# The tail of a graph network kernel: float16 halves, turns by products, 12 open output sums, tables added by DMA

## The chip, the cores and the metric

One NeuronCore of a Trainium2 chip runs the whole program as one launch. Its engines run beside each other and wait for each other through semaphores: TensorE (PE; its weight loads are listed as PEld), VectorE (DVE), ScalarE (ACT), GpSimd (POOL) and SyncE (SP, which here only issues transfers). TensorE writes to PSUM, a memory of 8 banks; the other data lie in SBUF, and large tables in DRAM. The metric is device time in microseconds (us). The time before is 2712.86 us, the median of three runs (2703.21 to 2717.07).

## The reference

A graph has N = 3125 nodes with 96 features and E = 100000 edges, sorted by destination. Four layers each add to x what they compute from h = relu(layernorm(x)): ten propagation hops (layer 0), a softmax-weighted neighbour sum and a product with W (layer 1), a message network with batch norms over the edges and a sum by destination (layer 2), and two graph convolutions (layer 3). The end of layer 2 and layer 3 are, in short:

```python
message = relu(concat(x[row], x[col], edge_feat) @ W_msg + b_msg)
mu = mean(message, 0); var = mean((message - mu)**2, 0)       # over the edges
message = g_msg * (message - mu) * rsqrt(var + 1e-5) + beta_msg
x = x + segment_sum(message, col) + node_feat

h = relu(layernorm(x))
dinv = rsqrt(deg)                     # in-degree plus the self loop
conv(h, W, b) = segment_sum((h @ W)[src] * dinv[src] * dinv[dst], dst) + b
t = conv(h, W1, b1); t = where(t > 0, t, a1 * t)
x = x + conv(t, W2, b2)
```

## The kernel before

**Tiles and tables.** The 3125 nodes are 25 blocks of 128 rows (`NB` = 25, `P` = 128), 3200 with padding. The counts of edges between all pairs of nodes are built once, as an 8-bit table in SBUF (`C8`, read as float8 `B8`, and its transpose `A8` for layer 0). A propagation or neighbour sum is then a matrix product: for each output block, 25 products of a 128x128 piece of the table with 192 columns of features. The 192 columns are a float16 number and a float16 remainder (`split`: the high half by ACT, the low half by DVE), which together stand for one float32 feature. The table is scaled, which the constant `FINE` = 512 undoes.

**Layers 0 to 2.** Layer 0 runs ten such products (`gather`, L400 on; its matmul is L409). At its end the pool "late" opens (from about L700): SP issues the weights of layers 1 and 2 one after the other, DVE fills a row of ones in `hTs` (L747), POOL writes an index pattern `li` (L761). Layer 1 (loop over the 25 blocks) runs two sums per block (L816), divides them, turns and multiplies by W1, and prepares the node tables `Pt` and `Qt` in DRAM; beside it the edge records are turned into fields (`in_fields`). Layer 2 then runs over units of four times 128 edges: edge features into the buffers `eh` and `el` (L1062 to L1065), messages (L1082), sums by destination (L1111, L1132), which go to one of two tables in DRAM, `Sd[0]` and `Sd[1]`, and a 97x194 product sum `gram` (L1100), from which come the mean and the mean square of the messages. That loop's order is written out by hand (`manual_schedule`). Everywhere else a planner orders the instructions of each engine: it takes the source's order as priority, has its own costs, and lets ready work go ahead of work that waits. It also keeps engines apart by whole PSUM banks: a write to a bank waits for earlier reads of that bank by other engines, whatever columns they touch.

**The tail, before.** After the loop `gram` is copied to `gs` (L1176). The pool "l3" takes SBUF that the message stage used, so its first tiles wait for that stage's last transfers. Then:

- the degree factor `dv` = rsqrt(degree + 1) for all nodes (L1185), by a bit trick and three Newton steps (`rsqrt`, L128 to L133);
- `sd` and `sd2`, the two tables, loaded by SP in five pieces of five blocks each (L1193) and added by POOL (L1194);
- the batch norm's mean and variance by four float32 products with ones (L1206, L1208), some ten DVE operations, a root, the factor `gr` and the shift `sh`;
- for five blocks at a time: the tables times `gr`, the shift times the degree, both added to x, and a layer norm (`norm`, L383 to L389), then per block `normed` (L394) and `weigh`: turn by a float32 transpose (L1227), copy (L1229), product with the float32 weight (L1231), scaled copy to `us` (L1232), and split into `u` (L398, L399);
- `gather` with `conv1` on each pair of output blocks: three DVE operations join the halves, the node's own feature (`us`) and the bias (L1238 to L1241), two make the leaky relu, then `weigh` with the second weight, and x gets the second bias (L1252);
- `gather` with `conv2`, which adds x and sends the block out (L1259).

Each PSUM tile "hop" is one bank and takes two output blocks, which are read after both have been summed. The pool of "hop" has three banks, "zp" and "op" two each.

## Time and profile before

| | |
|---|---|
| profiled execution, its own time | 2710.35 us |
| its span, first to last instruction | 2708.0 us |
| mean granted TensorE clock | 0.857 of full speed |
| busy share of the span | PE 68%, PEld 55%, DVE 55%, ACT 34%, POOL 32% |
| layer 1, about | 1575 to 1745 us |
| layer 2's edge loop, about | 1750 to 2532 us |
| set-up of layer 3 | 2532 to 2558 us |
| features of the 25 blocks | 2558 to 2586 us |
| first gather with conv1 | 2586 to 2651 us |
| second gather with conv2 | 2651 to 2702 us, last output landed by 2708 |

A row of a timeline gives the start, the duration, the engine, the line and operation, the tile written and the tile read, and in brackets how long the engine stood idle before it and what released it. A row of groups gives the busy time and the mean duration in ns, and behind the second bar the idle time of that engine ahead of those instructions. A duration includes a latency that the next independent instruction does not wait for, so starts are closer together than durations are long. A granted clock below 1 slows TensorE's products in proportion.

### The profile page before, as it was taken

The page shows a single profiled execution, that of the slowest core. Times are in us where ns is not written, and L with a number is a line of the kernel's source. Part 1 is how long each engine was busy: PE and PEld are TensorE (multiplying, and loading weights), DVE is VectorE, ACT ScalarE, POOL GpSimd, SP SyncE. Part 2 cuts the span into 40 slices and gives each one's busy share as a digit, 9 for nine tenths or more (in the row PEclk, how much of TensorE's full clock was granted, in tenths as well). Part 3 has the DMA queues.
Part 4 walks back from the last instruction along what each step waited for, and adds up shares of the span by engine and source line. Part 5 has one row for each costly group of instructions (what it writes and reads, how often), then busy time and mean ns, then how long its engine had stood idle before and what let it go on. Part 6 is the DMA issues. An engine that isn't in the chain of part 4 may idle for free. (4 is left out here: it accounts for less than half of the span.)

```text
span 2708.0 us, 51385 instructions
## 1 busy us (share of the span) xinstructions
PE 1844.3 (68%) x19447; PEld 1485.3 (55%) x19447; DVE 1480.2 (55%) x4400; ACT 919.6 (34%) x2334; POOL 870.8 (32%) x928
## 2 busy tenths in 40 slices
PE   0477777871375119314999989768777778788698
PEld 0223335760164008103999978656666666677588
DVE  3778999870045007101664677645655555556853
ACT  0488847370065003001331254223333323223340
POOL 4100000027723770774000000165555555545000
PEclk9889999985588559656999999878999989889799
DMA  4100000000000000000010021134344444334200
GB/s 119 56 9 1 1 1 3 8 10 4 4 9 9 4 4 10 5 4 5 11 26 2 2 51 34 34 95 103 93 106 103 104 101 102 92 95 96 60 1 20
DMA packets 133737, 108.21 MB, mean 40 GB/s; under 512 B 93607, under 2 KB 103341, under 8 KB 133479
## 3 DMA queue, kind: packets, MB, share of 16 engines
q1 hardware_dynamic: 106117, 79.60, 11.2%
q0 software_dynamic: 25952, 22.03, 4.4%
q8 instruction: 154, 2.52, 0.4%
q10 hardware_dynamic: 1410, 3.20, 0.4%
q14 instruction: 104, 0.85, 0.1%
HBM read 86.43 MB, written 18.29 MB: 39 GB/s over the span
## 5 line engine op out<-in xcount | busy, mean ns | idle before, releaser
L409 PE MATMUL hop<-u,A 128*128 128x192 f16 (+1 forms) x6250 | 618.1, 253 | 403.1 <-issue 398.5
L409 PEld LDWEIGHTS <-A 128*128 128x128 fp8e4 x6250 | 542.7, 99 | 492.2 <-issue 470.3
L1024 POOL DMA_INDIRECT h<-Pt,srow x408 | 418.0, 1024 | 505.2 <-PE pre L1082 226.5
L635 DVE SCALAR_TENSOR_TENSOR wt<-hop,sc,h 128x96 f32<-128x96 f32 x225 | 69.7, 310 | 575.6 <-remote 472.5
L555 POOL DMA_INDIRECT recs<-rec,x x250 | 245.6, 982 | 265.1 <-DVE wt L637 182.9
L668 ACT ACTIVATE eps<-eps 96x512 f32<-96x512 f32 x196 | 107.0, 570 | 586.8 <-remote 410.1
L1085 DVE SCALAR_TENSOR_TENSOR u<-pre,u 128x384 f16<-128x384 f32 x216 | 119.5, 553 | 327.6 <-ACT u L1084 267.0
L1084 ACT ACTIVATE u<-pre 128x384 f16<-128x384 f32 x216 | 105.9, 490 | 511.9 <-remote 204.7
L286 PE MATMUL cps<-hk,hl 128*128 128x500 f16 x784 | 231.3, 417 | 61.5 <-DVE hl L244 39.9
L1082 PE MATMUL pre<-W3h,eh 96*128 96x96 f16 x1728 | 230.5, 215 | 17.4 <-issue 17.3
L244 DVE TENSOR_TENSOR hk<-ki,keyT 128x4000 f16<-128x4000 f16 x98 | 219.7, 2242 | 35.7 <-PE cps L286 30.5
L1100 PE MATMUL gram<-u 128*97 128x194 f16 x864 | 200.4, 261 | 26.3 <-issue 25.8
L290 ACT ACTIVATE C<-cps 128x500 f32 x269 | 162.8, 605 | 99.5 <-PE cps L289 67.2
L1082 PE MATMUL pre<-W3h,el 96*128 96x96 f16 x864 | 184.6, 214 | 9.4 <-issue 9.0
L286 PEld LDWEIGHTS <-hl 128*128 128x128 f16 x784 | 73.7, 119 | 169.1 <-DVE hl L244 79.6
L555 POOL DMA_INDIRECT recs<-rec,addr x126 | 123.5, 981 | 106.9 <-DVE x L685 65.5
L1082 PEld LDWEIGHTS <-eh 96*128 96x128 f16 x1728 | 140.2, 103 | 22.2 <-issue 21.8
L1100 PEld LDWEIGHTS <-u 128*97 128x97 f16 x864 | 116.5, 135 | 64.8 <-issue 52.9
L1065 DVE SCALAR_TENSOR_TENSOR el<-ef,eh 96x512 f16<-96x512 f32 x216 | 147.5, 683 | 7.4 <-ACT eh L1064 5.9
L669 DVE BATCH_NORM_STATS2 x<-eps 96x6 f32<-96x512 f32 x196 | 134.5, 687 | 19.3 <-ACT eps L668 10.7
L1064 ACT ACTIVATE eh<-ef 96x512 f16<-96x512 f32 x216 | 126.7, 587 | 23.1 <-DMA spread<-fields 9.8
L1082 PE MATMUL pre<-qa,ohS 128*128 128x96 f16 x912 | 121.2, 210 | 14.5 <-issue 14.1
(427 smaller groups left out, 3738.4 us busy)
## 6 DMA issues: line engine op xcount, KB each, us to landing
spread<-fields SPq DMA_DIRECT2D x114, 256.0 KB
spread<-rl_d SPq DMA_DIRECT2D x51, 256.0 KB
h<-Pt,srow POOLq DMA_INDIRECT x408
recs<-rec,x POOLq DMA_INDIRECT x250
et<-fields SPq DMA_DIRECT2D x228, 9.0 KB
x<-ea_d SPq DMA_DIRECT2D x195, 18.0 KB
qg<-Qt SPq DMA_DIRECT2D x204, 12.0 KB
Sd<-zero SPq DMA_DIRECT2D x2, 1296.0 KB
```

The source lines that it names most:

```text
L244: V.tensor_tensor(t, pat[:, None, :, :].to_broadcast([P, s, n, c]), val[:, q, :].rearrange("p (s c) -> p s c", s=s)[:, :, None, :].to_broa ...
L286: T.matmul(ps, hl[:, j // 4, :, j % 4], hk[:, j // 2, :, j % 2], start=j == js[0], stop=n == 0 and j == js[-1])
L290: S.activation(C8[:, :, bass.ds(column_of(g), WIN)], ps, AF.Copy)
L409: T.matmul(ps[:, i, :], table[:, k, c0 + (b0 + i) * P:c0 + (b0 + i + 1) * P], u[:, k, :], start=k == 0, stop=k == NB - 1)
L555: ins = G.indirect_dma_start(out=recs[g], out_offset=bass.IndirectOffsetOnAxis(ap=addr[:, c0 + c:c0 + c + 1], axis=0), in_=r[:, c, :], in_ ...
L669: V.bn_stats(stats[:, i % 49, :], ps)
L1024: G.indirect_dma_start(out=pgs[i % len(pgs)][:, c, :], out_offset=None, in_=Pt, in_offset=bass.IndirectOffsetOnAxis(ap=srow[:, k:k + 1], a ...
L1064: S.activation(eh, ps[:D, :], AF.Relu)
L1065: V.scalar_tensor_tensor(el, ps[:D, :], 0.0, eh, ALU.max, ALU.subtract)
L1082: T.matmul(ps[:, c, :], t, w, start=j == 0, stop=j == len(by) - 1)
L1085: V.scalar_tensor_tensor(mm[:, :, D + 2:], ps, 0.0, mm[:, :, :D], ALU.max, ALU.subtract)
L1100: T.matmul(gram, mm[:, c, :D + 1], mm[:, c, :], start=n == 0 and c == 0, stop=n == L - 1 and c == HC - 1)
```

## The change

It concerns layer 3 and what leads to it.

- The weights, biases and slope of layer 3 are loaded at the start of layer 1, and the two weights are split into float16 halves there, in a pool that closes at the end of layer 1. The degree factor, its multiples (`dvF` = 512 dv, `dv2` = dv squared), two batch-norm constants (`cc`) and a scaled identity (`own`) are computed in layer 1, too. The memset of `hTs` goes from DVE to POOL.
- `eh` and `el` have two buffers instead of three; `gs` uses one of them.
- Mean and mean square come from one product of 192 columns; the three DVE operations ahead of it stand right behind the copy of `gram`.
- SP loads only `Sd[0]`; a transfer issued by POOL, which adds to what is there, brings `Sd[1]`. POOL's additions and `sd2` are gone.
- `weigh` splits the block before the turn: high half by ACT or DVE in turn, low half by DVE, two float16 products with an identity, one copy of 256 columns, three float16 products (high by high, high by low, low by high), then the high half of `u` by ACT and the low half by DVE, straight from PSUM. There is no `us` any more. Turn and result share one bank, of which there are two.
- The node's own feature: in the first convolution by one more product per output block with the scaled identity (`own`), 26 instead of 25; in the second one DVE operation in `weigh` adds it to x.
- `conv` is one ACT and one DVE operation, `conv1` adds the bias on DVE, `conv2` adds x on DVE; the second bias is added to x in `conv2`.
- The pool of "hop" has six banks. The first 12 output blocks have all their sums open at once (two per bank, started by a product with zeros), and each takes the products of feature block k right after that block's features are queued, one block late. After the last feature block come `conv1` of those 12, then the other 13 blocks, and the second gather, block by block: `done` is called after each block, not after each pair.
- The first group of blocks is of one block, the next of four, the rest of five.

```diff
-    V.memset(hTs[D:, :], 1.0)
+    G.memset(hTs[D:, :], 1.0)
+    soon = ExitStack()
+    where.append(soon.enter_context(tc.tile_pool(name="l1e", bufs=1)))
+    Wg = [load("W_g1", [D, D], a["L3_gnn_W1"]), load("W_g2", [D, D], a["L3_gnn_W2"])]
+    where.pop()
+    bg = [spread("L3_gnn_b1"), spread("L3_gnn_b2")]
+    a1 = spread("L3_gnn_a1", 1)
+    Wgh = [[where[-1].tile([D, D], F16, name=f"W_g{k}{i}") for k in "hl"] for i in range(2)]
+    for (hi, lo_), w in zip(Wgh, Wg):
+        split(hi, lo_, w)
...
+    V.tensor_scalar(own, ident16, 1.0 / FINE, None, ALU.mult)
...
+        V.tensor_scalar(dv, cnt_dst, 1.0, None, ALU.add)
+        V.tensor_copy(dv, rsqrt(dv, "rs_dv"))
+        V.tensor_scalar(dvF, dv, FINE, None, ALU.mult)
+        V.tensor_mul(dv2, dv, dv)
...
-            eh, el = (wp.tile([D, HC * P], F16, name=name) for name in ("eh", "el"))
+            eh, el = (wp.tile([D, HC * P], F16, name=name, bufs=2) for name in ("eh", "el"))
...
         V.tensor_copy(gs, gram)
+        V.scalar_tensor_tensor(mvar[:D, :], gs[:D, D + 2:], 2.0, gs[:D, :D], ALU.mult, ALU.add)
+        V.tensor_mul(sq[:D, D:], mvar[:D, :], ident[:D, :D])
+        V.tensor_add(sq[D:, :D], gs[D:, :D], gs[D:, D + 2:])
...
         for b in range(0, NB, 5):
-            for t, d in ((sd, Sd[0]), (sd2, Sd[1])):
-                nc.sync.dma_start(t[:, b:b + 5, :], d[b * P:(b + 5) * P].rearrange("(b p) d -> p b d", p=P))
-            G.tensor_tensor(sd[:, b:b + 5, :], sd[:, b:b + 5, :], sd2[:, b:b + 5, :], ALU.add)
+            t, d0, d1 = sd[:, b:b + 5, :], *(d[b * P:(b + 5) * P].rearrange("(b p) d -> p b d", p=P) for d in Sd)
+            nc.sync.dma_start(t, d0)
+            nc.gpsimd.dma_start(out=t, in_=d1, accum_op=ALU.add)
...
+        T.matmul(ps, ones[:D + 1, :], sq, start=True, stop=True)
...
         def weigh(i, b, t):
-            zp = qp.tile([P, P], F32, name="zp")[:D, :]
-            T.transpose(zp, t, ident)
-            zT = wp.tile([D, P], F32, name="zT")
-            S.activation(zT, zp, AF.Copy)
-            op = qp.tile([P, D], F32, name="op")
-            T.matmul(op, zT, Wg[i], start=True, stop=True)
-            S.activation(us[i][:, b, :], op, AF.Copy, scale=dv[:, b:b + 1])
-            split(u[i][:, b, :D], u[i][:, b, D:], us[i][:, b, :])
+            th = wp.tile([P, 2, D], F16, name="th")
+            if b % 2:
+                V.tensor_copy(th[:, 0], t)
+            else:
+                S.activation(th[:, 0], t, AF.Copy)
+            V.tensor_sub(th[:, 1], t, th[:, 0])
+            q = qp.tile([P, 2, 256], F32, name="zp")
+            zp, op = q[:D, 0, :], q[:, 1, :D]
+            for k in range(2):
+                T.matmul(zp[:, k * P:(k + 1) * P], th[:, k], ident16, start=True, stop=True)
+            zT = wp.tile([D, 2, P], F16, name="zT")
+            S.activation(zT.rearrange("p a b -> p (a b)"), zp, AF.Copy)
+            for n, (k, w) in enumerate(((0, 0), (0, 1), (1, 0))):
+                T.matmul(op, zT[:, k], Wgh[i][w], start=n == 0, stop=n == 2)
+            S.activation(u[i][:, b, :D], op, AF.Copy, scale=dv[:, b:b + 1])
+            V.scalar_tensor_tensor(u[i][:, b, D:], op, dv[:, b:b + 1], u[i][:, b, :D], ALU.mult, ALU.subtract)
+            if i:
+                V.scalar_tensor_tensor(x[:, b, :], op, dv2[:, b:b + 1], x[:, b, :], ALU.mult, ALU.add)
+        def part_of(i, b, k, ps, first, stop=True):
+            T.matmul(ps, B8[:, k, PAD + b * P:PAD + (b + 1) * P], u[i][:, k, :], start=first, stop=i == 1 and k == NB - 1)
+            if i == 0 and k == NB - 1:
+                T.matmul(ps, own, u[i][:, b, :], start=False, stop=stop)
+        def conv(b, ps):
+            lo = wp.tile([P, D], F32, name="cs")
+            S.activation(lo, ps[:, D:], AF.Copy, scale=dvF[:, b:b + 1])
+            t = wp.tile([P, D], F32, name="co")
+            V.scalar_tensor_tensor(t, ps[:, :D], dvF[:, b:b + 1], lo, ALU.mult, ALU.add)
+            return t
...
+        OPEN = 12
+        early = [pp.tile([P, 2, 256], F32, name="hop") for _ in range(OPEN // 2)]
...
+        def parts(k):
+            for b in range(OPEN):
+                part_of(0, b, k, early[b // 2][:, b % 2, :2 * D], False, b % 2 == 1)
-        for b0 in range(0, NB, 5):
+        for b0, n in ((0, 1), (1, 4)) + tuple((b, 5) for b in range(5, NB, 5)):
...
                 weigh(0, b, hb)
-        gather(pp, B8, u[0], conv1, c0=PAD)
-        gather(pp, B8, u[1], conv2, c0=PAD)
+                if b:
+                    parts(b - 1)
+        parts(NB - 1)
+        for b in range(OPEN):
+            conv1(b, early[b // 2][:, b % 2, :2 * D])
+        for i, done, bs in ((0, conv1, range(OPEN, NB)), (1, conv2, range(NB))):
+            for b in bs:
+                if b % 2 == 0:
+                    ps = pp.tile([P, 2, 256], F32, name="hop")
+                for k in range(NB):
+                    part_of(i, b, k, ps[:, b % 2, :2 * D], k == 0)
+                done(b, ps[:, b % 2, :2 * D])
```

## The prediction

> **What bounds the kernel now.** I read the page's slices first, then the tail stretch by stretch, then the timeline at the seams and the chain that ended last. Stretches (columns: length, busy time and count of PE, weight load, DVE, ACT, POOL, then granted clock, DMA share, GB/s):
>
> ```profile
> 2532.00:2558.00 26.00, 2.48 (x10) 1.90 (x9) 21.50 (x91) 0.25 (x1) 6.49 (x5) 0.56 0.42 101
> 2558.00:2575.00 17.00, 13.84 (x86) 10.72 (x87) 15.77 (x109) 15.17 (x59) 0.00 (x0) 0.77 0.01 2
> 2575.00:2585.00 10.00, 7.79 (x61) 5.79 (x59) 6.99 (x43) 9.53 (x39) 0.00 (x0) 1.00 0.01 2
> 2600.00:2620.00 20.00, 20.00 (x218) 18.61 (x218) 9.82 (x46) 6.34 (x23) 0.00 (x0) 1.00 0.01 2
> 2660.00:2680.00 20.00, 20.00 (x242) 20.00 (x241) 7.04 (x30) 0.00 (x0) 0.00 (x0) 1.00 0.08 21
> ```
>
> The tail has three limits. Up to 2558 it is a DVE chain with PE nearly idle. From 2558 to 2586 ("the ramp") the 25 blocks become features, and ACT is busy throughout. After that TensorE is full to the end. The groups of the ramp (2558 to 2586), then the seams from the timelines and the chain:
>
> ```profile
> L394 ACT ACTIVATE hb<-x,ln_m,ln_r 128x96 f32<-128x96 f32 x25 | 10.8, 458 | 25.9 <-DVE ln_m L389 25.9
> L1232 ACT ACTIVATE us<-op,dv 128x96 f32<-128x96 f32 x25 | 8.0, 333 | 2.0 <-PE op L1231 1.8
> L1229 ACT ACTIVATE zT<-zp 96x128 f32<-96x128 f32 x25 | 6.4, 264 | 0.2
> L398 ACT ACTIVATE u<-us 128x96 f16<-128x96 f32 x25 | 6.0, 274 | 0.1
> L409 PE MATMUL hop<-u,C 128*128 128x192 f16 x72 | 11.6, 266 | 2.1 <-DVE u L399 2.1
> ```
>
> ```profile
> 1575.85 5.39 DVE L747 MEMSET hT<- 1x6400 f16 x1 [1.39 <-issue]
> 1583.35 2.58 PE L816 MATMUL hop<-u,C 128*128 128x192 f16 x15 [4.83 <-DVE ebn_r L133]
> 2536.02 8.40 SPq L1193 DMA_DIRECT2D sd<-Sd  x10
> 2539.98 1.19 POOL L1194 TENSOR_TENSOR sd<-sd,sd 128x480 f32<-128x480 f32 x1 [41.40 <-DVE mvar L1213]
> 2540.00 1.29 DVE L1214 TENSOR_TENSOR mvar<-mean,mvar 128x96 f32<-128x96 f32 x1
> 2558.08 1.18 ACT L394 ACTIVATE hb<-x,ln_m,ln_r 128x96 f32<-128x96 f32 x3 [25.63 <-DVE ln_m L389]
> 2586.26 5.80 PE L409 MATMUL hop<-u,C 128*128 128x192 f16 x48 [0.63 <-DVE u L399]
> 2651.14 50.00 PE hop L409 x596
> ```
>
> A DVE memset holds TensorE 4.83 us at the start of layer 1. At 2540 a DVE operation that elsewhere takes 0.26 us takes 1.29 beside POOL's addition. The second gather runs 596 products in 50.0 us: 0.084 us each. From 2586.26 to the last product (2701.40) the tail takes 115.1 us; 11% of that is not gather, namely 25 float32 turns and products, about 0.52 us a block (two blocks cycle in 5.22 us, of which 50 products take 4.18).
>
> **The change part by part.** The sum goes against the profiled execution: span 2708.0, time 2710.35, which is 2.5 us below the median 2712.86. A difference under 0.5% (13.6 us) I call no change: about what a measurement of this kernel can tell.
>
> Start of layer 1: the 5.39 us memset moves to POOL. The wait of 4.83 us goes; the granted clock of 1583 to 1590, 0.52 after that idle time, could give up to 3.5 more. What is late next: weights whose last load SP issues at 1579.88, and about 0.9 us of new DVE work (splitting two weights, a scaled identity, a memset). Five loads of 0.47 us move on SP ahead of the record loads (2.35 us); those feed the field turning, from block 2 on. POOL's memset, some 5.5 us by its 0.92 us for 1000 elements a row, is first read by a product at 1596.8; the index pattern queued behind it on POOL is used only from 1748. TensorE is busy 37.1 of 40 us from 1600, so a gain here reaches the end. Bounds 0 to -8.3; I take -4, near the wait itself. The degree chain (some 16 operations of 0.18, 3 us) moves into layer 1, where DVE is busy 29.6 of 40 us: nothing, or +3 if it fell on the path. Two buffers instead of three for the edge features: nothing, because the products that read a buffer stand on TensorE ahead of the product that refills it.
>
> Set-up: today the Gram copy at 2532.29 leads to the first block at 2558.08. DVE waits 3.2 us for a write before the degree chain, two pairs of float32 products take 1.14 and 1.17, and five POOL additions stretch DVE operations. New chain: copy 0.36, three operations 0.7, one product 1.2, scaling 0.36, five operations at 0.29, eleven of the root at 0.29, one more: the factor is there at 2540. The tables: SP may issue at 2536.02 as now; two tables of five blocks had landed by 2539.98, so one by about 2539. Then POOL issues the adding transfer. No row shows one. Plain POOL transfers of 28 KB take 0.58 to issue; a gather of 128 rows comes every 1.25 and five of these make the 640 rows, 6.2 us. With some 3 us to land, the first five blocks are there between 2542.5 and 2548; I take 2543.5, near the plain transfer, the same kind of instruction. The later four hide behind a ramp that uses five blocks in 8 us, by either price. A group of one block needs about 15 dependent operations of 0.2, so its first activation is at about 2546.5: -11.6.
> The Trainium skill's page "SBUF — State Buffer", "Who interferes with whom", speaks against POOL here: GpSimd cannot write its descriptors while DVE works in a two-port mode. This trace has POOL issues of usually 0.94 and once 2.32 us (at 2493.42) beside DVE; 1.4 us more on the first transfer would make the sum 2689.
>
> Ramp: per block ACT keeps 0.458 for the activation and 0.333 for the scaled copy; the turned copy doubles (0.264 for 128 columns, 0.58 for 512: about 0.37) and a copy falls on every second block (0.14): 1.30 against 1.33, paced today at 1.12. DVE needs 0.95 per block for the norms today (start to start); new are a subtraction (0.17), half a copy (0.09) and the low half from PSUM (0.24): 1.45. So DVE becomes the limit, and the turn now holds one of two PSUM banks from the first product to the low half: five steps of 0.41, 0.47, 0.38, 0.44 and 0.41 (a row's duration, products with 0.25 latency, and 0.1 for the handover), 2.1 us before any queueing. I add 0.3 of queueing at each of the four later steps: 3.3, or 1.65 per block. I take 1.65: the end is 2546.5 + 41.3 = 2587.8 against 2586.26, +1.5. Bounds: 1.45 (2582.8) and 2.0 (2596.5). TensorE's own load, 12 x 0.084 + 0.24 = 1.24 per block, hides below that; if the clock stays at 0.5 it does not.
>
> After the ramp: 24 products remain of the 12 open blocks, 13 x 26 = 338 of the others and 625 of the second gather: 987 x 0.0836 = 82.5 us. Turns in float16: 2 x 0.054 + 3 x 0.043 = 0.24 us (spacing of the 128- and 96-column float16 rows), 25 times 6.0. That is 88.5. Add 2.0 until the first open bank is read and free, and 4.0 for the next part: 94.5 against 115.1, -20.6. DVE's 25 new conv1 blocks, about 1.45 each or 36 us, run beside TensorE's 36.3 of that stretch: a near tie, not on the path.
> Bank waits: two blocks share a bank and the even one is now drained before the odd one may be written: product latency 0.25, ACT 0.33, DVE 0.31 and handovers, 1.2 us in 18 places. The planner can put the next pair's first products there, as it puts turns among products today; I count 0.2 for each, bounds 0 and 1.2.
> End: a sum on ACT, then two DVE operations, for three on DVE: +0.3.
>
> Sum: -4 + 1.5 - 20.6 + 0.3 = -22.8: 2687.5, and 2688 as the measured time.
>
> **Rivals.**
> Better than that: the ramp at DVE's pace (-5), the whole of layer 1's stall (-4), no bank waits (-4): about 2674. For: the scheduler already mixes independent work well. Against: DVE would be without a gap for 36 us.
> Banks: nothing fills the 18 waits: +17.6, about 2705. For: today both blocks of a bank are read after both are written, so no row shows such a fill. The Trainium skill's "PSUM — Partial Sum Buffer", section on bank collisions, has the same rule: guard by bank, not by address, so the wait is real; only its cover is open, and no row here shows it.
> The open sums don't run early: the planner leaves 288 products behind the ramp, 24 us back, about 2711. Against: 72 products already ran inside the ramp.
> The other side: the two turn banks set the pace in both stages. With a round of R us, the ramp takes 12.5 R and the first-layer outputs 2 + 12.5 R. At R = 4.0 the end is where it is now; at 4.6 it is 0.5% later; at R = 5, every step waiting longer than it works, the ramp ends at 2609 and the whole at about 2734. For: the steps lie on three in-order queues, DVE full. Against: the work itself is 2.1 us, and waits of a full length at every step are not seen in today's ramp, where ACT waits 2 us in 28.
>
> **How the numbers follow.** Forecast (2678 to 2698) 0.55; better 0.17; banks 0.12; sums not early 0.05; slow banks 0.11, of it 0.08 beyond 0.5%. Faster by over 0.5% (below 2699): 0.55 + 0.17 = 0.72; within: 0.12 + 0.05 + 0.03 = 0.20; slower 0.08. The range 2668 to 2710 holds forecast, better and banks and leaves out some 0.16.
>
> **What would show it.** Start of layer 1: no idle TensorE near 1580, the next seam some 4 us earlier. Set-up: no 1.1 to 1.3 us DVE operations; first activation 12 us after the Gram copy instead of 26. Ramp: over 250 hop products inside it, DVE busiest, 1.65 us a block. Then TensorE full, about 94 us to the last product, with short waits on ACT or DVE at odd blocks. Wrong if TensorE waits over 1 us at each odd block, if a turn's round takes over 4 us, or if an adding transfer takes more than 8 us to land.

## The result, and the profile after

The changed kernel takes 2700.32 us (median of 20 runs, 2691.63 to 2711.6) against 2712.03 us for the kernel before (20 runs beside them). The ratio is 0.9959, interval 0.9944 to 0.9973: 11.7 us less, where 22.8 were forecast (2687.5 against the 2710.35 of the profiled execution). The time lies inside the stated range, but the gain is half of the forecast one. The profiled execution is the lowest of the 20 (2691.63 us, span 2689.4), so its span can't be set against that of before; only its parts can. From the Gram copy (`gs`) to the end the trace has 165.0 us, the one of before 175.7: 10.7 us of the gain are in the tail. Layer 1 gained nothing.

Stretches of the changed kernel (length, busy time and count of PE, weight load, DVE, ACT, POOL, then granted clock, DMA share, GB/s). The Gram copy is at 2524.41; the stretches are the set-up, the start and the rest of the ramp, the first and the second gather:

```profile
2524.00:2542.00 18.00, 3.63 (x10) 1.16 (x9) 15.42 (x81) 0.25 (x1) 7.76 (x5) 0.58 0.92 142
2542.00:2560.00 18.00, 14.66 (x137) 12.00 (x138) 16.64 (x110) 12.15 (x38) 0.00 (x0) 0.76 0.04 6
2560.00:2585.00 25.00, 23.06 (x279) 20.16 (x277) 13.13 (x67) 16.62 (x51) 0.00 (x0) 1.00 0.01 2
2600.00:2620.00 20.00, 19.41 (x231) 16.63 (x228) 17.04 (x89) 10.04 (x35) 0.00 (x0) 1.00 0.01 2
2660.00:2680.00 20.00, 19.55 (x227) 18.81 (x225) 5.76 (x20) 3.07 (x10) 0.00 (x0) 1.00 0.09 24
```

The set-up is 18 us instead of 26. In the first 18 us of the ramp VectorE is the busiest engine (16.6 us, TensorE 14.7); in the other 25 it is TensorE, with 23 us, and VectorE is at half. In the two gathers TensorE is no longer quite full: 19.4 and 19.6 of 20 us, where it had 20.0. The timeline at the start of layer 1:

```profile
1572.22 5.43 POOL L747 MEMSET hT<- 1x6400 f16 x1 [312.33 <-ACT exs L651]
1573.44 4.26 DVE L761 TENSOR_SCALAR own<-ident 128x128 f16<-128x128 f16 x1
1573.75 3.96 DVE L129 TENSOR_SCALAR ebn_r<-ebn_r_t 96x1 int32<-96x1 int32 x1
1573.84 6.19 DVE L797 COPY cnt<-cnt_dst 128x25 f32<-128x25 f32 x1
1577.72 2.27 POOL L781 IOTA li<- 128x1024 f16 x1
1577.76 2.26 DVE L131 TENSOR_TENSOR ebn_r_t<-ebn_r 96x1 f32<-96x1 f32 x1
1582.33 0.96 PE L836 MATMUL hop<-u,C 128*128 128x192 f16 x5 [4.76 <-DVE both L841]
```

The memset is on POOL, and VectorE stands just as long: operations that take some 0.15 us elsewhere last until POOL's memset ends at 1577.65, and a copy that started beside them, with what stands behind it, until POOL's index pattern ends at 1579.99. TensorE idles 4.76 us instead of 4.83. The set-up and the seam to the ramp:

```profile
2524.41 0.36 DVE L1205 COPY gs<-gram 97x194 f32<-97x194 f32 x1
2528.16 3.06 SPq L1217 DMA_DIRECT2D sd<-Sd  x5
2531.45 0.26 DVE L1231 TENSOR_TENSOR gr<-rs_msg,s_L_gnn_g_msg 128x96 f32<-128x96 f32 x1
2531.72 7.76 POOL L1218 DMA_DIRECT2D sd<-Sd  x5 [43.34 <-DMA sd<-Sd]
2536.69 0.73 DVE L1300 TENSOR_TENSOR sd<-sd,gr 128x96 f32<-128x96 f32 x2 [1.06 <-DMA sd<-Sd]
2539.43 0.65 DVE L1300 TENSOR_TENSOR sd<-sd,gr 128x480 f32<-128x480 f32 x1
2542.47 0.47 ACT L394 ACTIVATE hb<-x,ln_m,ln_r 128x96 f32<-128x96 f32 x1 [17.89 <-DVE ln_r_t L132]
```

The factor `gr` is there 7.3 us after the copy, but the first tables only 12.3 and the first activation 18.1 us after it. Between the tables and that activation VectorE works on the second and third group of blocks too (the 480 columns at 2539.43). No DVE operation of 1.1 to 1.3 us is left in the set-up.

The groups of the tail (2531 to 2690):

```profile
L1258 PE MATMUL hop<-u,C 128*128 128x192 f16 x1250 | 126.2, 248 | 4.3 <-DVE u L1252 2.6 <-DVE co L1267 0.8
L1248 ACT ACTIVATE zT<-zp 96x256 f16<-96x256 f32 x50 | 18.1, 377 | 13.0 <-PE zp L1246 12.5
L1251 ACT ACTIVATE u<-zp,dv 128x96 f16<-128x96 f32 x50 | 16.3, 337 | 7.0 <-PE zp L1250 6.3
L1252 DVE SCALAR_TENSOR_TENSOR u<-zp,dv,u 128x96 f16<-128x96 f32 x50 | 15.8, 315 | 16.3 <-ACT u L1251 16.1
L394 ACT ACTIVATE hb<-x,ln_m,ln_r 128x96 f32<-128x96 f32 x25 | 11.2, 458 | 19.0 <-DVE ln_r_t L132 17.9 <-DVE th L1242 0.7 <-DVE ln_m L389 0.3
```

The times of single steps are near the estimates (zT 0.377 where 0.37 was taken, u 0.337, the low half 0.315). The 25 first activations wait once for long, at the set-up (17.9 of 19.0 us); after that ACT waits mostly for products.

### The profile page after: what moved, and what is told of

Read it like the earlier page. It is cut to its first block, busy times and chain, and to the rows that moved or that the text cites. A ratio compares the mean times of both kernels' runs of the same rounds, so it can differ in the third digit from the quotient of the medians.

```text
span 2689.4 us, 51768 instructions
## 1 busy us (share of the span) xinstructions
PE 1835.7 (68%) x19572; PEld 1477.4 (55%) x19572; DVE 1490.5 (55%) x4471; ACT 936.3 (35%) x2362; POOL 884.2 (33%) x929
## 5 line engine op out<-in xcount | busy, mean ns | idle before, releaser
L1053 POOL DMA_INDIRECT h<-Pt,srow x408 | 423.9, 1039 | 484.5 <-PE pre L1111 212.3
L1111 PE MATMUL pre<-W3h,eh 96*128 96x96 f16 x1728 | 229.4, 214 | 16.9 <-issue 16.7
L1111 PEld LDWEIGHTS <-eh 96*128 96x128 f16 x1728 | 139.3, 103 | 21.5 <-issue 20.9
L1111 PEld LDWEIGHTS <-ohS 125*128 125x128 f16 (+1 forms) x1824 | 112.9, 102 | 36.1 <-issue 32.7
```

The source lines that it names most:

```text
L1053: G.indirect_dma_start(out=pgs[i % len(pgs)][:, c, :], out_offset=None, in_=Pt, in_offset=bass.IndirectOffsetOnAxis(ap=srow[:, k:k + 1], a ...
L1111: T.matmul(ps[:, c, :], t, w, start=j == 0, stop=j == len(by) - 1)
```

## The experiments

All experiments change one or a few places of the changed kernel (one starts from the kernel before), and none leaves any work out. Some ran on chips on which the kernel before takes 2022 to 2026 us instead of about 2713 (the last section says where that lies). The table calls the slower kind A and the faster kind B; B is three chips (e1 to e4, e5 to e8, e13 to e15). A ratio is always against runs of the kernel before beside it, and the table sets parts of single traces side by side. Its columns, in us: layer 1, from its first activation (`hb<-x,m,r`) to its last product with the counts (`weighed<-cnt,hb`); the message loop, from there to the Gram copy; then, counted from the Gram copy, the first use of the tables, the first activation of layer 3, the first `conv` of an output block, the start of the last product, and the end of the span. On B TensorE also waits 21 to 22 us in every run up to layer 1's first activation, which the column leaves out.

```
kernel                 chip  layer 1   loop | tables  act.   conv  last p.   end | ratio
before                  A     169.7   789.1 |  15.8   25.8   58.0   168.6  175.7 |
changed                 A     171.3   780.5 |  12.3   18.1   61.3   158.5  165.0 | 0.9959
changed, again (e12)    A     171.7   798.0 |  12.2   17.9   61.5   158.3  164.8 | 0.9953
e1 memset on DVE        B     170.8   566.8 |  12.2   18.0   61.2   158.4  164.9 | 0.9941
e2 row by block         B     166.3   569.4 |  11.7   17.5   60.2   157.8  164.3 | 0.9910
e3 first tables         B     172.4   566.7 |   9.9   16.4   59.8   156.5  163.0 | 0.9949
e4 bank each            B     172.2   565.8 |  12.4   18.2   61.6   155.5  161.9 | 0.9919
e5 lag two              B     172.4   563.8 |  12.1   17.9   57.5   154.4  161.3 | 0.9941
e6 sums late            B     171.5   567.0 |  12.3   18.1   57.2   153.8  160.6 | 0.9950
e7 float32 turns        B     172.6   567.0 |  12.1   17.9   63.3   164.2  170.8 | 0.9987
e8 before, POOL memset  B     170.3   565.7 |  17.1   26.1   56.6   167.3  174.6 | 1.0015
e9 no open sums         A     171.3   796.1 |  12.3   18.1   54.0   175.1  181.9 | 1.0017
e10 set-up order        A     171.9   787.6 |   9.9   15.1   64.0   160.9  167.5 | 0.9955
e11 five edits          A     166.0   795.6 |   9.9   15.2   59.7   153.6  160.3 | 0.9909
e13 no open, own bank   B     172.4   571.9 |  12.1   17.9   53.3   163.9  170.5 | 0.9997
e14 three edits         B     165.7   566.6 |  12.4   18.1   58.4   152.5  159.3 | 0.9896
e15 four edits          B     165.7   566.7 |   9.9   16.4   56.9   150.7  157.3 | 0.9883
```

The intervals of the ratios are 0.0012 to 0.0035 to either side, 2 to 7 us, and are given where a verdict rests on one. The parts from the Gram copy on are steadier: three traces of the same tail (changed, e12, e1), on both kinds of chip, have it at 164.8 to 165.0. So effects of a few us are read from the parts.

**The memset.** The theory: POOL's memset holds VectorE.

```diff
-    G.memset(hTs[D:, :], 1.0)
+    V.memset(hTs[D:, :], 1.0)                       # e1
```

> The changed kernel with the memset of hTs back on VectorE, all else as changed. Theory: a POOL memset holds VectorE for as long as it lasts (in the changed kernel VectorE's operations of 1573.4 to 1573.8 last 4 to 6 us, until POOL's 5.43 us end), so the move gained nothing: TensorE's idle time at the start of layer 1 stays at 4.7 to 4.9 us and the time is that of the changed kernel within 2 us (ratio to the kernel before about 0.996). Rival: the move did gain its 4 us and something later ate it: then this kernel is 4 us later than the changed one at the end of layer 1, ratio about 0.9975.

Ratio 0.9941 (0.992 to 0.9963), layer 1 170.8 us. The ten runs with the memset on POOL and otherwise the same layer 1 have 171.3 to 172.6, so by this one trace the move cost some 1 us; it gained none. The theory's number for TensorE's idle time missed: 2.3 us, not 4.7 to 4.9. That one wait is no steady measure: the changed kernel itself has 4.76 in one trace and 3.2 in the other (e12), and e3 has 3.2 on a faster chip. The rival, that the move brought 4 us which were lost later, falls with layer 1's length.

```diff
-    G.memset(hTs[D:, :], 1.0)
...
+            V.memset(hT(0, b * P, P)[D:, :], 1.0)   # e2, per block of layer 1
             S.activation(hT(0, b * P, P, D), zp, AF.Copy)
```

> The changed kernel with no long memset at all: each block of layer 1 writes its own 128 ones ahead of its use, some 0.15 us on VectorE 25 times. Theory (the long memset, on either engine, is what TensorE waited for): TensorE's idle time at the start of layer 1 falls from 4.76 us to under 1.5, and layer 1 ends 3 to 5 us earlier after the last product of layer 0 than in the changed kernel; ratio to the kernel before about 0.994 to 0.9945. Rival (the weights that SP loads until 1579 or the root of the edge norm are late anyway): TensorE still idles 3 us or more there, gain under 1.5 us.

Layer 1 takes 166.3 us, 5 to 6 us less than with the memset on POOL; three more runs with this edit have 166.0, 165.7 and 165.7. TensorE has no wait over 0.4 us left where it had stood. The timeline of this kernel there:

```profile
1111.50 0.17 DVE L863 MEMSET hT<- 1x128 f16 x1
1115.36 0.66 PE L835 MATMUL hop<-u,C 128*128 128x192 f16 x6
1116.35 0.29 PE L850 MATMUL zp<-ident,z 128*96 128x128 f32 x1 [0.33 <-issue]
1116.48 0.67 PE L835 MATMUL hop<-u,C 128*128 128x192 f16 x6
```

Each block's ones cost 0.17 us, and the wait is gone (on a slower chip, e11, one of 1.8 us is left of it): the long memset was its main cause, on either engine. In this run the message loop took 569.4 us, some 3 more than in its neighbours, which looked like a gain given back; e14 and e15 have the same layer 1 and loops of 566.6 and 566.7, so that was chance.

```diff
-    V.memset(hTs[D:, :], 1.0)
+    G.memset(hTs[D:, :], 1.0)                       # e8, in the kernel before
```

> The kernel before with one edit, the memset of hTs on POOL. Theory (POOL's memset holds VectorE, and POOL's index pattern, now behind it, holds it again for its 2.3 us): layer 1, from the first to the last of its per-block steps, takes 167.5 to 169 us, 1 to 2 us longer than before (166.8); ratio 1.0 to 1.001. Rival (as forecast): 162 to 164 us, ratio about 0.998. It also shows the message loop with three buffers of edge features: from layer 1's last block to the Gram copy within 3 us of the 566 to 569 us that the four runs with two buffers took.

Ratio 1.0015 (0.9998 to 1.0032): this part alone gains nothing in the kernel before either. By the table's measure layer 1 came out at 170.3 us against 169.7 before, 0.6 longer where 1 to 2 were expected, and not 3 to 5 shorter as by the rival (whose 166.8 for the kernel before is counted between other steps). The loop with three buffers took 565.7 us, inside the 563.8 to 571.9 of those with two: no cost of the buffers shows, as forecast.

**The set-up.**

```diff
             nc.sync.dma_start(t, d0)
-            nc.gpsimd.dma_start(out=t, in_=d1, accum_op=ALU.add)
+            if b == 0:
+                sd2 = lp.tile([P, 5, D], F32, name="sd2")
+                nc.sync.dma_start(sd2, d1)
+                V.tensor_add(t, t, sd2)
+            else:
+                nc.gpsimd.dma_start(out=t, in_=d1, accum_op=ALU.add)   # e3
```

> The changed kernel, but the first five blocks' tables come by two plain loads of SP and one VectorE addition; the other four pieces still by the adding transfers. Theory (the adding transfers are what was late in the set-up: issued by POOL from 2531.72, landed 2536.7, while the factor gr was ready at 2531.7): the first activation comes 12.5 to 15 us behind the Gram copy instead of 18.1, and the last features 3 to 5 us earlier against that copy; time 3 to 5 us less than the changed kernel. Rival: the later adding transfers or TensorE's cold clock pace the first blocks anyway, and the last features move by less than 1.5 us.

The tables come 2.4 us earlier (9.9), but the first activation only 1.7 (16.4), outside the expected 12.5 to 15: 6.5 us lie between tables and activation, where the changed kernel has 5.8, with VectorE at work for the later groups as well. The last features and the first `conv` move by 1.5 us and the end by 2.0, between the 3 to 5 of the theory and the less than 1.5 of the rival.

```diff
+            with tc.issue_after(lead[0]) if lead else ExitStack():   # lead: last DVE step of the first group's norm
                 V.tensor_mul(sd[:, g, :], sd[:, g, :], over_b(gr, n))
                 V.tensor_add(x[:, g, :], x[:, g, :], sd[:, g, :])
                 r, m = norm(b0, n)                                   # e10, on top of e3
```

> The changed kernel with the first five tables by plain loads, as in the earlier run, and with VectorE's work for the later groups of blocks queued behind the last operation of the first group's norm. Theory (VectorE's order is the second half of the late start: the first activation comes 5.8 us behind the first tables because 20 operations of later groups stand among the 15 of the first): the first activation comes 3.5 to 4.5 us behind the first tables, at 13.3 to 14.5 us behind the Gram copy instead of 18.1, and the last product starts 3 to 5 us earlier than 158.5 us behind it. Rival (what is put behind only makes the second group late): the first activation comes earlier, but the last product moves by less than 2 us, as in the run with the plain loads alone (156.5).

The first activation comes at 15.1, later than the expected 13.3 to 14.5, and the end 2.5 us later than in the changed kernel (167.5), 4.5 later than with the plain loads alone. The rival was right and too mild. ACT's first two rows of layer 3 in this trace:

```profile
2544.47 0.47 ACT L396 ACTIVATE hb<-x,ln_m,ln_r 128x96 f32<-128x96 f32 x1 [14.97 <-DVE ln_m L391]
2552.33 1.18 ACT L396 ACTIVATE hb<-x,ln_m,ln_r 128x96 f32<-128x96 f32 x3 [5.08 <-DVE ln_m L391]
```

The second block comes 7.9 us behind the first; in the changed kernel it was 2.1 (2542.47, 2544.58). The other groups' steps among the first group's were not waste: here the first block came early and the next four late, and the end was later.

**The ramp and the open sums.**

```diff
-                if b:
-                    parts(b - 1)
-        parts(NB - 1)
+                if b > 1:
+                    parts(b - 2)
+        parts(NB - 2)
+        parts(NB - 1)                                # e5
```

> The changed kernel with the open sums taken two feature blocks behind instead of one. Theory (in the ramp TensorE's order makes it wait for the low half of the block just turned: idle 0.2 to 0.36 us at half of the blocks, a block takes 1.53 us where TensorE's own work is 1.24): the block falls to 1.25 to 1.4 us, the conv of the first open block begins 57 to 60 us behind the Gram copy instead of 61.3, the end 2 to 4 us earlier. Rival (the two turn banks or ACT and VectorE pace the ramp): the block stays at 1.5 us or more, the end within 1 us of the changed kernel's 165.0 us behind the Gram copy, or later by the 12 products that now stand behind the ramp (1.0 us).

The first `conv` comes at 57.5 instead of 61.3 and the end 3.7 us earlier: TensorE's own order, with products queued that still wait for the block just turned, paced the later ramp (2.3 us of such waits in the changed kernel between 2552 and 2585, none in this one; that the other 1.5 us lie in what stood behind them is not shown). Over the last 15 blocks a block now takes 1.41 us, against 1.54, which just misses the expected 1.25 to 1.4.

```diff
-                if b:
-                    parts(b - 1)
-        parts(NB - 1)
+        for k in range(NB):
+            parts(k)                                 # e6, behind the loop over the blocks
```

> The changed kernel with all products of the 12 open sums behind the last features instead of among them. Theory (the ramp is TensorE's since it carries 288 products there, 24.1 us at 0.0836): without them a block takes 1.1 to 1.35 us, the features end 4 to 10 us earlier, and 24 us of products come behind: the end 14 to 20 us later than the changed kernel's 165.0 us behind the Gram copy. Rival (the ramp is paced by the chain of a block through two turn banks, so the early products are nearly free): the ramp keeps its 42.7 us, and the end is 22 to 25 us later.

Both theories missed the end: the tail is 4.4 us shorter than in the changed kernel. Of these 300 products 230 still ran ahead of the last features (288 in the changed kernel), and 292 ahead of the first `conv`, as many as before: the planner takes source order as priority and pulls ready products forward. With the lowest priority they fill what the turns leave, and the last features come at 52.2 us instead of 60.7. So this is no test of what open sums are worth, but a better order for them. The first 18 us of this ramp:

```profile
1863.10:1881.10 18.00, 16.12 (x169) 13.05 (x170) 17.00 (x109) 14.06 (x48) 0.00 (x0) 0.83 0.01 3
```

VectorE is busy 17.0 of 18 us here, TensorE 16.1. The test of the open sums:

```diff
-        OPEN = 12
-        early = [pp.tile([P, 2, 256], F32, name="hop") for _ in range(OPEN // 2)]
...                                                   # e9: and parts(), the 12 conv1 calls
-            tc.tile_pool(name="l3p", bufs=6, space=PSUM) as pp
+            tc.tile_pool(name="l3p", bufs=3, space=PSUM) as pp
-        for i, done, bs in ((0, conv1, range(OPEN, NB)), ...
+        for i, done, bs in ((0, conv1, range(NB)), ...
```

> The changed kernel without the 12 open sums: three PSUM banks for the products as before, all 25 output blocks summed one after the other, float16 turns and set-up as changed. It answers what the open sums bring, which the kernel with their products written behind the ramp could not: there the planner ran 292 products inside the ramp all the same. Theory (they bring what TensorE can do during the ramp): at most 100 products run in the ramp, the features end 5 to 10 us earlier than the changed kernel's 60.8 us behind the Gram copy, some 16 us of products come later, and the last product starts 164 to 170 us behind the Gram copy instead of 158.5. Rival (nearly free either way): 157 to 161.

72 products run in the ramp, the features come 7.1 us earlier, and the last product starts at 175.1, 16.6 us later, beyond the expected 164 to 170. The end, at 181.9, is 6.2 us later than in the kernel before, in spite of the shorter set-up and cheaper turns. Ratio 1.0017 (1.0003 to 1.0031). Most of this kernel's ramp:

```profile
2560.40:2592.10 31.70, 24.09 (x167) 17.62 (x168) 27.01 (x163) 24.45 (x79) 0.00 (x0) 0.52 0.01 2
```

The granted clock is 0.50 for 30 us of the ramp, where the changed kernel has it for 8 us and then 1.00. VectorE is the busiest engine, 27.0 of 31.7 us, so the clock need not be what kept the lighter ramp from being faster in proportion. In the first 18 us of the ramp VectorE is busy 16.4 to 17.1 us in e5, e6, e9 and e13 alike, and each has ten or eleven blocks done after them, with 107, 106, 30 and 62 of the early products beside the turns and a clock of 0.77, 0.83, 0.50 and 0.78: there neither the number of products nor the clock set the pace.

```diff
-                if b % 2 == 0:
-                    ps = pp.tile([P, 2, 256], F32, name="hop")
+                ps = pp.tile([P, 2, 256], F32, name="hop")
...
-                    part_of(i, b, k, ps[:, b % 2, :2 * D], k == 0)
-                done(b, ps[:, b % 2, :2 * D])
+                    part_of(i, b, k, ps[:, 0, :2 * D], k == 0)
+                done(b, ps[:, 0, :2 * D])            # e4; e13 is e9 with this and six banks
```

> The changed kernel with one output block per PSUM bank in everything behind the 12 open sums (13 blocks of the first gather, all 25 of the second); the 12 open ones still share. Theory (the drain of the even block is what costs: a pair of output blocks of the second gather takes 4.43 us in the changed kernel, where the 50 products need 4.18): a pair takes 4.18 to 4.2 us, and the stretch from the last features to the last product falls from 97.9 us to 93 to 95; time 3 to 5 us less. Rival (the wait is for output buffers or is the product rate itself): a pair stays at 4.4 us and the stretch within 1 us of 97.9.

From first `conv` to last product it takes 93.9 us instead of 97.2; 93 to 95 were expected from the last features, and these were 94.5. ACT's rows for the output blocks of the second gather, first of the changed kernel:

```profile
2664.10 0.34 ACT L1265 ACTIVATE cs<-hop,dvF 128x96 f32<-128x96 f32 x1 [2.69 <-PE hop L1258]
2665.50 0.34 ACT L1265 ACTIVATE cs<-hop,dvF 128x96 f32<-128x96 f32 x1 [1.06 <-PE hop L1258]
2668.53 0.34 ACT L1265 ACTIVATE cs<-hop,dvF 128x96 f32<-128x96 f32 x1 [2.69 <-PE hop L1258]
2669.93 0.34 ACT L1265 ACTIVATE cs<-hop,dvF 128x96 f32<-128x96 f32 x1 [1.06 <-PE hop L1258]
```

then with a bank for each block:

```profile
1981.91 0.34 ACT L1265 ACTIVATE cs<-hop,dvF 128x96 f32<-128x96 f32 x1 [1.75 <-PE hop L1258]
1984.00 0.34 ACT L1265 ACTIVATE cs<-hop,dvF 128x96 f32<-128x96 f32 x1 [1.75 <-PE hop L1258]
1986.09 0.34 ACT L1265 ACTIVATE cs<-hop,dvF 128x96 f32<-128x96 f32 x1 [1.75 <-PE hop L1258]
```

A pair took 4.43 us (2664.10 to 2668.53), of which 0.25 are the wait for the even block's drain; alone, a block takes 2.09, exactly 25 products of 0.0836.

> The changed kernel without the open sums (25 output blocks one after the other), but with one block per PSUM bank and six banks, where the earlier run without open sums had three banks of two blocks. Theory (what a shared bank costs is the wait for the even block's drain, here at all 25 pairs): the last product starts 6 to 9 us earlier than that run's 175.1 us behind the Gram copy, at 166 to 169. Rival (banks cost little when the open sums are gone; the turns' products in TensorE's order cost the rest): less than 4 us, 171 to 175.

The last product starts at 163.9 instead of 175.1, more than the theory asked. But the run changed two things: with six banks instead of three the planner also found room for 147 products ahead of the first `conv` instead of 75, and 72 products are 6.0 us; the first `conv` came 0.8 earlier. That leaves 4.4 us for the drains of shared banks, here 24 pairs, against 3.3 for 18 in e4: 0.18 a pair on average in both. The 16.6 us of e9 then read: 217 products fewer ahead of the first `conv`, +18.1; first `conv` 7.3 earlier; and 5.8 for longer waits of TensorE behind it. Summed over the distances of its starts, less their usual spacing, these waits are 8.9 us in the changed kernel and 14.7 in e9: by what the trace names as released last, 1.3 more for drains, some 3.5 more for the halves `th` of a turn and 0.8 more for ACT's copy of a turned block. e13 ends 5.5 us behind the changed kernel.

**The turns.**

```diff
-            (th: two halves, two float16 products, zT of 256 columns, three float16 products)
+            T.transpose(zp, t, ident)
+            S.activation(zT, zp, AF.Copy)
+            T.matmul(op, zT, Wg[i], start=True, stop=True)            # e7
```

> The changed kernel with the old turn: a float32 transpose, a float32 copy of 128 columns, one product with the float32 weight; all else as changed (the weights are loaded at the start of layer 1, and not split). Theory (behind the ramp TensorE is full, so a turn costs what it takes there: about 0.5 us in float32 against 0.24): the stretch from the last features to the last product is 5 to 8 us longer than the changed kernel's 97.2; the ramp, where TensorE has some 0.3 us to spare per block and the split's three steps are gone, moves by less than 4 us either way. Rival (the split's extra steps on ACT and VectorE cost as much as TensorE saves): the end is within 2 us of the changed kernel's 165.0 us behind the Gram copy, or earlier.

The end is 5.8 us later, so the rival falls: the float16 turns earn about half of the tail's gain. But only 3.7 of the 5.8 lie behind the first `conv` (100.9 us against 97.2, below the expected 5 to 8), and 2.0 in the ramp. Per turn behind the ramp that is 0.15 us, where the prediction had 0.28 (0.52 less 0.24).

**Together.** Five edits (e2, e3, e4, e6, e10), on a chip of the slower kind, with the changed kernel itself beside them:

> The changed kernel with five edits together: ones written per block in layer 1, one output block per bank behind the open sums, the open sums' products written behind the ramp, the first tables by plain loads, VectorE's later groups behind the first norm. If the terms add: layer 1 about 5 us shorter, of which 2 to 3 reach the Gram copy; from the Gram copy to the end 165 - 3.4 - 4.4 - 2 = 155 us (153 to 158); ratio to the kernel before about 0.988 (0.985 to 0.991). If the ramp is TensorE's whatever the start, the set-up's part is lost: 157 to 159 us.

> The changed kernel itself, unedited, as the base for the runs beside it. From the Gram copy to the end 165.0 us (164.5 to 165.5), ratio to the kernel before 0.993 to 0.996.

Ratio 0.9909 (0.9891 to 0.9927) for the five, 0.9953 (0.9937 to 0.9969) for the changed kernel. The tail, 160.3, missed the 155 (153 to 158). The set-up's order, which e10 had shown to cost, is the suspect; without it:

> The changed kernel with three edits: ones written per block in layer 1, one output block per bank behind the open sums, the open sums' products written behind the ramp; the set-up as changed. Theory (it was VectorE's order in the set-up that cost the combined kernel): from the Gram copy to the end 156 to 158 us, against 160.3 of the combined kernel and 164.8 of the changed one; layer 1 166 to 167 us; ratio to the kernel before 0.988 to 0.991. Rival (the three tail edits do not add): 159.5 us or more.

> The same with the first five tables by plain loads and one VectorE addition. Theory (the plain loads bring 1 to 2 us also here): from the Gram copy to the end 154.5 to 156.5 us, ratio 0.987 to 0.990. Rival (TensorE's own work is the ramp, whatever its start): within 0.5 us of the kernel with three edits.

Three edits (e2, e4, e6): tail 159.3, between the two expectations, so e4 and e6 do not quite add (5.7 of 7.5 us). With the plain loads (e3) as the fourth: 157.3, another 2.0 as expected, though not the 154.5 to 156.5 that had been put on it. It differs from the five edits by the set-up's order alone, and its tail is 3.0 us shorter. Its ratio is 0.9883 (0.9861 to 0.9905), 23.7 us less than the kernel before. That is the lowest ratio of this study, and about the gain that had been forecast for the change itself.

## Why the prediction was right or wrong

The direction was right, and the size was double. By the traces of before and after the sum is +1.6 (layer 1), +6.8 (set-up and ramp), -16.9 (behind the features), -0.6 (end): -9.1, against -4, +1.5, -20.6 and +0.3. So 13.7 us of the forecast did not come: 5.6 in layer 1, 5.3 up to the last features and 3.7 behind them, less 0.9 at the end. A gain of 9.1 lies inside the interval of the measured one (7.3 to 15.2); the message loop, 8.6 us shorter in the one trace, is left out for the reason given in the last section.

- **Start of layer 1: the step that failed outright.** "The wait of 4.83 us goes" took VectorE as free once the memset was POOL's. The trace after has VectorE's operations standing beside it for its whole length, and then beside POOL's index pattern for 2.26 us more, which the prediction had passed over since its result is used late. Price: 5.6 us. That the memset's removal is worth the wait, and reaches the end, is right: 5 to 6 us of layer 1 (e2, e14), and e11's median lies 12.6 us below e12's beside it, of which its tail explains 4.5. The Trainium skill's page "SBUF — State Buffer", "Who interferes with whom", has the rule: VectorE and GpSimd share a port pair, and for VectorE's two-port modes "Whoever issues first gets the shared pair for the whole instruction", while the other is blocked; it names copies and `tensor_scalar` among the operations that can enter these modes. The trace agrees: the `tensor_scalar` on 128x128 float16 lasted 4.26 us, ending with POOL's memset. The prediction had weighed this section for transfers only.
- **The degree chain and the buffers: nothing**, right for the buffers (565.7 us against 563.8 to 571.9). The chain wasn't tried alone; with the memset on DVE, layer 1 is 1.2 us longer than before, on different chips.
- **Set-up: the start -7.7 instead of -11.6.** The factor was on time (7.3 us, 7.7 forecast), the tables 1.1 us later than taken. The plain table had landed 7.3 us behind the copy, not the 6.7 taken, and from there the adding transfer took 5.0 us, not 4.5; it takes 1.55 us to issue (7.76 for five), nearer the gather's price than the plain transfer's 0.58 that was chosen. The larger part, 2.8 us, is "about 15 dependent operations of 0.2": VectorE ran 27 operations of later groups among the 17 of the first, and they took 5.8 us together. e10 shows that this isn't to be had by order alone.
- **Ramp: 42.7 us forecast as 41.3, with half of the reason.** VectorE at 1.45 per block and two turn banks were to be the limit. In the first 18 us VectorE was the busiest engine (16.6 us), and runs with 30 to 107 early products there all had ten or eleven blocks done, against eight in the changed kernel; so for this part VectorE's limit is not refuted. In the other 25 us it was busy 13, and TensorE 23, in an order that queued products ahead of their features; "hides below that" was said of just that load. e5 and e6 brought the first `conv` 3.8 to 4.2 us forward by order alone. That the total came out near the forecast was luck in part: what paces the ramp with that order mended was not tested.
- **Behind the features: 97.7 instead of 94.5.** The mis-sized term is the turn, "2 x 0.054 + 3 x 0.043 = 0.24 us". In 2590 to 2632 TensorE issued 383 products of the sums (32.0 us at 0.0836) and 21.5 turns in 42 us: 0.46 us a turn. The products' spacings were right, their waits were put at nothing: 4.7 us in this stretch, of which 2.5 lie ahead of the weight products, where TensorE stands until ACT's copy is there, 0.9 ahead of the turning products, 0.9 behind them, and 0.3 elsewhere, the bank waits among it. Over 25 turns that is 5.5 us more than the 6.0 taken. What had 2.0 (first open bank) and 4.0 (bank waits) together cost some 4, of it 3.3 for the banks (e4).
- **Rivals.** "Banks", with all 18 waits unfilled at 17.6 us, did not come: 0.25 us per pair of the second gather were left uncovered, 3.3 in all (e4), and 4.4 over 24 pairs where there were no open sums (e9 against e13). "Open sums not early": 288 products ran in the ramp, as forecast ("over 250"). "Two turn banks set the pace" at R = 4 or more: two blocks took 3.4 us over the whole ramp and 3.1 over its last 15 blocks, so no. (Its 2734 at R = 5 also left out the 4 us taken for layer 1.)
- **What would show it.** Right: no stretched operations, over 250 products in the ramp, the short waits at odd blocks. Wrong: no idle TensorE in layer 1. VectorE as the busiest engine held for the first 18 us of the ramp alone. That list also had the first activation at 12 us behind the copy, where the working had 14.2; it came at 18.1.

## What to carry to other kernels

Before a long operation is moved to an idle engine, look which other engine stands still beside that one's operations in the trace; here it was cheaper to cut the memset into 0.17 us pieces. When an engine is to be filled with early work, try that work at the lowest priority: queued in front of the work that feeds it, it cost 4.4 us here. Price a chain by the queue it stands in, not by its own operations alone.

## What the runs showed that was not expected

- **Two kinds of chip, one program.** The kernel before took about 2713 us on some chips and 2022 to 2026 on others. The products of layer 0 show it. First the changed kernel on a slower chip, then e3, whose layer 0 is the same, on a faster one (groups: busy time, mean ns, then idle time ahead):

```profile
L409 PE MATMUL hop<-u,A 128*128 128x192 f16 (+1 forms) x6250 | 615.7, 253 | 403.8 <-issue 398.4
```

```profile
L409 PE MATMUL hop<-u,A 128*128 128x192 f16 (+1 forms) x6250 | 550.1, 247 | 4.8 <-DVE u L399 2.3 <-DVE wt L637 1.9 <-issue 0.3
```

On the slower chip TensorE stops 235 times for up to 3.2 us ("issue": nothing in the trace that it waits for), 398 us in all; on the other, it doesn't. Of these 398 us 388 lie in stretches where the granted clock is 0.50, which make up 532 of layer 0's 1125 us; the mean clock there is 0.76, against 0.98 on the faster chip. The first stops, from 593 us on, stand some 5 us ahead of the first such long stretch, so the low clock may as well follow from them. What stops TensorE can't be told from these traces. The message loop differs in the same way (780 to 798 us against 564 to 572), while the tail is equal to 0.2 us. That may be why the runs on the slower chips scatter by 20 us. The loop of one and the same kernel took 780.5 and 798.0 us (changed and e12), so the 8.6 us between the profiles of before and after can't be put down to the change.

- **A lighter ramp at half clock.** In the changed kernel the granted clock was 0.50 until 8 us after the first activation and 1.00 from then on. With 72 instead of 288 products beside the turns it was 0.50 for 30 us (e9, same kind of chip); with 144 products it was 0.50 for 7 us, 1.00 for 10, 0.50 for 3, and 1.00 for the last 14 us (e13, faster chip). But the kernel before, with 72 products beside float32 turns, had 1.00 from 8 us on as well. So early products may also pay for the clock of the turns, but their number alone does not decide it, and these runs do not give the rule.
